# A mixture of eight experts computed for the chosen tokens only, in tiles of 128, between the half steps of an attention loop

## The chip, the cores and the metric

The kernel runs on one NeuronCore of one Trainium2 chip, in float32 throughout. The metric is the device time of one execution in microseconds (us), lower being better. Engines are named as the profile names them: PE multiplies matrices (PEld is its loading of weights), DVE and POOL work element by element, ACT evaluates functions and copies, and SP only issues transfers. POOL also issues the transfers that gather or scatter rows by a list of row numbers. Each engine works through its own instructions in order.

## The reference

There are eight sequences (batches) of 512 tokens with 256 channels. Cut to its parts, the reference is

```python
x = x + over_heads(masked_attention(x))         # stage A: 16 heads; then attention among the heads of one token
y = mixture(x)                                  # stage B, first mixture
x = x + second_mixture(layernorm(y + mha(y)))   # stage B: 16 heads of 16; stage C: one of 8 experts per token

def mixture(x):                                 # T = 4096 tokens, E = 8, two experts per token
    scores = softmax((x @ wt.T + repeat(g @ wg.T, 512)) / 2)
    w, idx = top_k(scores, 2);  w = w / (w.sum(-1) + 1e-20)
    up = leaky(x @ w_gate[e]) * (x @ w_up[e])    # for each e: 256 -> 128, leaky slope 0.01
    y_all[e] = up @ w_down[e]                    # 128 -> 256
    y = sum of w[t, c] * y_all[idx[t, c], t] over c = 0, 1
    return y + (leaky(x @ sw_gate) * (x @ sw_up)) @ sw_down   # a shared expert, width 256
```

The second mixture has its own router, experts of width 512 with a ReLU, and a layernorm after the sum.

## The kernel before

The kernel has three stages, each with its own pools of tiles, one after another.

**Stage A** is the masked attention and the attention among a token's heads ("over-heads"). A flag read at run time picks one of two programs. The mask keeps keys only in the last quarter of a sequence here, so `late_keys` (from line 733) runs: 16 units, each one sequence and half the heads, whose steps are written out by hand. Into their gaps `aside` pulls steps of an iterator `side` (line 981), which is `over_heads_here` (801): one over-heads piece for a row common to most tokens, then `rest` (793), which stores x for the first three quarters of every sequence, then `over_heads()`, which takes pieces from the list `oh_todo` until it is empty. A piece (`one_over_heads`, 187) is 128 tokens in 29 steps: a few matmuls, and 16 large products on POOL (line 244), each followed by a reduction on DVE (247). `hand_over` (332) puts the last 128 tokens of a sequence on the list after stage A has computed them, for the first `BESIDE` = 3 sequences; the other five are worked off in stage B. x after stage A lies in device memory as columns 0 to 255 of `rows_d`.

**Stage B** is the first mixture and 16-head self-attention. `begin(b)` (1300) prepares a batch. `experts` (1246) transposes its tokens, `route` (1173) computes scores and a weight for every token and expert, zero except for two, and then the shared expert and all eight experts are applied to all 512 tokens (`gated`, 1207; products at 1211, 1218 and 1272), each result multiplied by its weight and added into y by DVE (1275). The weights of all experts are loaded once, at the start of the stage. `begin` goes on with the transposed y, the values and the first group's queries and keys. The attention is the loop over 256 half steps, 32 for a batch: a head group `n` of four heads takes eight. In each half step `both` (1365) issues four score matmuls side by side in the array, two for a row maximum (`nmz`, DVE, 1338) of a later group and two whose exponential (`pT_s`, ACT, 1363) is taken; `gather` (1377) multiplies exponentials and values; `divide` (1400) sends sums of the softmax through device memory and back, four small transfers on SP, and multiplies; `end` (1422) is the output projection, layernorm and the second router, whose choice `hand_on_to` scatters into a list of tokens by expert.

The order is by hand. After each half step's attention work, the loop pulls as many steps of `side`, the chained `begin(b)` of all later batches at 38 steps each, as a table `room` gives for that place in the batch; `late`, the left over-heads pieces, gets three or four steps. `begin(0)` and two projections run before the loop. All PSUM tiles of the side work share three banks (`ps_m`).

**Stage C** is the second mixture in the sparse form: tokens sorted by expert in tiles of 256; each tile's tokens gathered from `rows_d` by POOL with a list that SP has loaded (1594, 1597), its expert's weights loaded by SP (1606 to 1610) at an address read from a table in a register, the results scattered to the output. The table is computed by 22 small DVE instructions from the number of tokens for each expert.

Of the kernel before, what the change touches and what calls it, by code (L numbers as in the profile page):

```python
# [24 lines left out]
E = 8  # L25
# [6 lines left out]
ROW = 2 * D + 16  # L32
LAST = NT - 1
BESIDE = 3
# [3 lines left out]
def tile_adaln_attn_ffn(ctx: ExitStack, tc: tile.TileContext, a: dict, out: bass.AP):  # L38
# [67 lines left out]
    rows_d = dram.tile([B * S, ROW], F32, name="rows", tag="rows")  # L106
    w_chosen = mid.tile([P, KD, 12], F32, name="wr", tag="wr")
# [18 lines left out]
    )  # L126
    sofar = mid.tile([P, NT + 1, E], F32, name="sofar", tag="sofar")
    nc.gpsimd.memset(sofar, 0.0)

# [57 lines left out]
    def one_over_heads(i, b, row=None):  # L187
# [4 lines left out]
        if row is None:  # L192
            rows = slice(b * S + i * P, b * S + (i + 1) * P)
            cn = ohp.tile([P, D], F32, name="cn", tag="cn", bufs=3)
            nc.sync.dma_start(cn, cn_d[rows, :])
            xi = ohp.tile([P, D], F32, name="xi", tag="xi", bufs=2)
            nc.sync.dma_start(xi, a["x"][b, i * P : (i + 1) * P, :])
        else:
            cn = row
# [78 lines left out]
        nc.sync.dma_start(rows_d[rows, 0:D], xo)  # L278
        oh_done[b] += 1
# [52 lines left out]
    def hand_over(i, b, pc, mv, rs):  # L332

        cn = ohp.tile([P, D], F32, name="cn_out", tag="cn", bufs=3)
# [398 lines left out]
    def late_keys():  # L733


        with ExitStack() as ph:
# [56 lines left out]
            def rest(b):  # L793
# [4 lines left out]
                nc.sync.dma_start(rows_d[b * S : b * S + LAST * P, 0:D].rearrange("(t p) c -> p t c", p=P), xi)  # L798
                oh_done[b] += LAST

            def over_heads_here():
# [5 lines left out]
                yield from over_heads()  # L807
# [196 lines left out]
            for _ in chain(prep, side, over_heads()):  # L1004
# [25 lines left out]
    def first_max(pool, src, rank, tag):  # L1030
# [4 lines left out]
        oh = pool.tile([p, n, w], F32, name="fm_o" + tag, tag="fm_o" + tag)  # L1035
# [5 lines left out]
        return oh, m  # L1041

    def choose(wk, ps, tag, xT):
# [14 lines left out]
        def best(l, rank, tag):  # L1058
# [9 lines left out]
            return first_max(wk, l, rank, tag)  # L1068
# [51 lines left out]
    with ExitStack() as ph:  # L1120
# [24 lines left out]
        wge, wue, wde = [], [], []  # L1145
        for e in range(E):
            wge.append(wload(f"wge{e}", a["w_gate"][e], P))
            wue.append(wload(f"wue{e}", a["w_up"][e], P))
            wde.append(load(f"wde{e}", [P, D], a["w_down"][e]))
# [16 lines left out]
        v_sets = [wp.tile([P, NT, H * VW + 32 - VW], F32, name=f"v{u}", tag=f"v{u}") for u in range(2)]  # L1166
# [6 lines left out]
        def route(b, xT):  # L1173

            gb = wk.tile([64, P], F32, name="gb", tag="gb")
# [16 lines left out]
            o1, m1 = first_max(wk, sc, rank8, "1")  # L1192
            s2 = wk.tile([P, NT, E], F32, name="r_s2", tag="r_s2")
            nc.vector.scalar_tensor_tensor(s2, o1, -2.0, sc, ALU.mult, ALU.add)
            o2, m2 = first_max(wk, s2, rank8, "2")
# [4 lines left out]
            nc.vector.tensor_tensor(m1, m1, den, ALU.mult)  # L1200
            nc.vector.tensor_tensor(m2, m2, den, ALU.mult)
            nc.vector.tensor_tensor(o1, o1, bc(m1, 2, E), ALU.mult)
            nc.vector.tensor_tensor(o2, o2, bc(m2, 2, E), ALU.mult)
            nc.vector.tensor_tensor(o1, o1, o2, ALU.add)
            return o1

        def gated(xT, wg_, wu_):
# [4 lines left out]
            hh = wk.tile([P, S], F32, name="hh", tag="hh", bufs=3)  # L1212
# [25 lines left out]
        x1 = {}  # L1238

        def load_x1(b):  # L1240
            x1[b] = wk.tile([P, NT, D], F32, name="x1", tag="x1")
            r = b * S
            assert oh_done[b] == NT
            nc.sync.dma_start(x1[b], rows_d[r : r + S, 0:D].rearrange("(t p) c -> p t c", p=P))

        def experts(b, y):

            xT = transposed(wk, ps_m, x1.pop(b), "x1T", ps_tag="m")
            yield
            cw = route(b, xT)  # L1250
            yield
            hs = []
            for c in range(2):
                h = yield from gated(xT, swg[:, :, c * P : (c + 1) * P], swu[:, :, c * P : (c + 1) * P])
                hs.append(h)
# [10 lines left out]
            for e in range(E):  # L1266
                h = yield from gated(xT, wge[e], wue[e])
                for u in range(2):
# [533 lines left out]
```

## Time and profile before

| | us |
|---|---|
| median of three runs (2145.59 to 2154.9) | 2146.6 |
| the profiled execution | 2142.55 |
| its span, first to last instruction | 2140.8 |
| PE busy | 1746.2 (82%) |
| DVE busy | 1104.6 (52%) |
| POOL busy | 536.5 (25%) |
| ACT busy | 502.0 (23%) |

The core's mean granted PE clock is 0.887 of full speed. In a row of the profile, "out<-in" names the tiles written and read, "x" the count, then come busy time in us, the mean of one in ns, and after the bar the idle time of the engine just before these instructions with what ended it. A float32 matrix product appears as two MATMUL records. Busy PE time counts overlapped records once.

### The profile page before, as it was taken

The numbers are of one execution on the slowest core, as the hardware profiler recorded it, in microseconds if no ns is written. First come the engines' busy times: TensorE is split into PE (matmuls) and PEld (weight loads), VectorE is DVE, ScalarE is ACT, GpSimd is POOL, SyncE is SP. The second block draws the span as 40 slices with busy tenths as digits, with TensorE's granted clock in tenths as the row PEclk, the third lists the DMA queues.
The fourth block names the chain that finished last, engine by engine and source line by source line (L and its number), as shares of the span: only waits on it lengthen the run. The fifth ranks groups of instructions, "written<-read, shape, count | busy, mean of one in ns | idle before, by whom it ended". The sixth has DMA issues, their size and how long they took to land.

```text
span 2140.8 us, 21024 instructions
## 1 busy us (share of the span) xinstructions
PE 1746.2 (82%) x7552; PEld 903.4 (42%) x7552; DVE 1104.6 (52%) x2563; ACT 502.0 (23%) x887; POOL 536.5 (25%) x539
## 2 busy tenths in 40 slices
PE   4898224899899988998999999999998885476775
PEld 3665113443343433443444344444443322465664
DVE  4865441456666554564555565564555441343433
ACT  1444000012222122322222323322323322010000
POOL 2510560013233320020010010010010022277677
PEclk9999556969999989999999999998998978688887
DMA  4210005000000000000000000000000000444441
GB/s 133 62 53 13 10 19 146 0 3 18 6 13 4 3 14 11 2 12 11 2 1 22 2 1 12 2 2 12 2 1 12 2 12 4 141 145 145 150 134 49
DMA packets 92145, 74.22 MB, mean 35 GB/s; under 512 B 36285, under 2 KB 81853, under 8 KB 92032
## 3 DMA queue, kind: packets, MB, share of 16 engines
q1 hardware_dynamic: 75200, 58.49, 9.1%
q0 software_dynamic: 6912, 12.88, 2.0%
q10 hardware_dynamic: 9920, 1.42, 0.4%
q8 instruction: 61, 1.00, 0.2%
q14 instruction: 52, 0.43, 0.1%
HBM read 61.95 MB, written 16.42 MB: 37 GB/s over the span
## 4 chain that ended last, share of the span: by engine, by line
PE 61%; DVE 13%; POOL 11%; DMA 6%; issue 4%; ACT 1%; SPq 1%; POOLq 0%; DVEq 0%; ACTq 0%
PE pss L1335 12%; PE pg L1211 6%; PE po_s L1384 6%; PE pu L1218 5%; PE pd L1272 5%; POOL pr L244 4%; DVE nmz L1338 3%; PE pq_s L1289 3%; PE px_s L1428 2%; PE pk_s L1295 2%; PE pst L1359 2%; PE py L1654 2%; DMA sums<-oT_s 2%; DMA xg<-rows,ids_j 2%; PE prs L1418 2%
## 5 line engine op out<-in xcount | busy, mean ns | idle before, releaser
L1338 DVE TENSOR_REDUCE nmz<-pss 128x2 f32<-128x1024 f32 x256 | 311.9, 1220 | 228.9 <-PE pst L1359 192.7
L1363 ACT ACTIVATE pT_s<-pst 128x1024 f32<-128x1024 f32 x256 | 261.8, 1024 | 593.4 <-PE pst L1359 593.4
L1335 PE MATMUL pss<-k_s,q_s 32*128 32x512 f32 x1024 | 327.5, 685 | 69.1 <-DVE nmz L1338 68.6
L1359 PE MATMUL pst<-q_s,k_s 32*128 32x512 f32 x1024 | 310.1, 676 | 1.9 <-DVE nmz L1338 1.6
L1433 POOL TENSOR_TENSOR y<-y,bo_bc 128x256 f32<-128x256 f32 x32 | 23.2, 725 | 838.1 <-DVE y L1432 838.1
L1335 PEld LDWEIGHTS pss<-k_s,q_s 32*128 32x128 f32 x1024 | 86.2, 193 | 260.3 <-DVE nmz L1338 119.8
L1384 PE MATMUL po_s<-pT_s,v 128*32 128x512 f32 x1024 | 157.4, 626 | 4.5 <-ACT pT_s L1363 4.5
L244 POOL TENSOR_TENSOR pr<-qk 128x512 f32<-128x512 f32 x72 | 88.5, 1263 | 211.4 <-DVE fm_r L1039 117.7
L1272 PE MATMUL pd<-wde,hh 128*128 128x256 f32 x512 | 127.4, 392 | 15.5 <-DVE hh L1219 14.6
L1211 PE MATMUL pg<-x1T,wge 128*128 128x512 f32 x256 | 126.0, 616 | 5.2 <-DVE q_s L1351 2.7
L1275 DVE SCALAR_TENSOR_TENSOR y<-pd,fm_o,y 128x256 f32<-128x256 f32 x256 | 109.6, 478 | 37.6 <-PE pd L1272 36.7
L1218 PE MATMUL pu<-x1T,wue 128*128 128x512 f32 x256 | 122.4, 600 | 0.0
L1272 PEld LDWEIGHTS pd<-wde,hh 128*128 128x128 f32 x512 | 94.1, 192 | 63.7 <-DVE hh L1219 32.5
L244 POOL TENSOR_TENSOR pr<-at,v_h 128x512 f32<-128x512 f32 x72 | 89.2, 1275 | 97.7 <-DVE at L259 74.1
L1654 PE MATMUL py<-w,h_e 128*128 128x256 f32 x368 | 108.2, 460 | 0.0
L1214 DVE TENSOR_TENSOR hh<-hh,pg 128x512 f32<-128x512 f32 x80 | 54.6, 683 | 95.5 <-ACT hh L1213 95.4
L1654 PEld LDWEIGHTS py<-w,h_e 128*128 128x128 f32 x368 | 86.8, 242 | 15.7
L1213 ACT ACTIVATE hh<-pg 128x512 f32<-128x512 f32 x80 | 47.7, 597 | 194.4 <-PE pg L1211 185.0
L1628 PE MATMUL pt_j<-ident,xg 128*128 128x128 f32 x92 | 21.9, 347 | 87.0 <-DMA xg<-rows,ids_j 86.9
L1359 PEld LDWEIGHTS pst<-q_s,k_s 32*128 32x128 f32 x1024 | 80.9, 191 | 22.3 <-issue 13.1
L1639 PE MATMUL ph<-xTj,w 128*128 128x256 f32 x368 | 85.1, 385 | 0.8 <-DVE xTj L55 0.8
L1639 PEld LDWEIGHTS ph<-xTj,w 128*128 128x128 f32 x368 | 71.0, 193 | 11.3 <-DVE xTj L55 1.2
(266 smaller groups left out, 2564.5 us busy)
## 6 DMA issues: line engine op xcount, KB each, us to landing
w<-in_w_dram SPq DMA_DIRECT2D x46, 512.0 KB
rows<-xr SPq DMA_DIRECT2D x8, 544.0 KB
x<-rows SPq DMA_DIRECT2D x8, 512.0 KB
x_rest<-in_x_dram SPq DMA_DIRECT2D x8, 384.0 KB
rows<-x_rest SPq DMA_DIRECT2D x8, 384.0 KB
b<-in_b_dram SPq DMA_DIRECT2D x23, 128.0 KB
wq<-in_Wq_dram SPq DMA_DIRECT2D x1, 1024.0 KB
wo<-in_Wo_dram SPq DMA_DIRECT2D x1, 1024.0 KB
```

Of the source, the lines that this page charges most:

```text
L244: nc.gpsimd.tensor_tensor(pr, x, y, ALU.mult)
L1211: nc.tensor.matmul(pg, wg_[:, k, :], xT[:, k, :], start=(k == 0), stop=(k == KD - 1))
L1218: nc.tensor.matmul(pu, wu_[:, k, :], xT[:, k, :], start=(k == 0), stop=(k == KD - 1))
L1272: nc.tensor.matmul(pd[:, t, :], h[:, q : q + P], wde[e], start=True, stop=True)
L1275: nc.vector.scalar_tensor_tensor(yt, pd[:, t, :], cw[:, 2 * u + t, e : e + 1], yt, ALU.mult, ALU.add)
L1335: nc.tensor.matmul(pss[:, u, :], qs[n][r, t * P : (t + 1) * P], ks[n][r, :], start=True, stop=True)
L1338: return lambda: nc.vector.tensor_reduce(nmz[n % 2].rearrange("p t (h r) -> p t h r", h=4)[:, t, 2 * pr : 2 * pr + 2, HD], pss, AX.X, ALU.max,
L1359: nc.tensor.matmul(pst[:, u, :], ks[n][r, c * P : (c + 1) * P], qs[n][r, :], start=True, stop=True)
L1363: return lambda: nc.scalar.activation(pT, pst, AF.Exp)
L1384: nc.tensor.matmul(pos[n][hd * 32 : hd * 32 + 32, :], v_sets[b % 2][:, c, (4 * g + hd) * VW : (4 * g + hd) * VW + 32], ws[hd // 2][:, hd % ...
L1639: nc.tensor.matmul(ph_, w1[:, k, c * P : (c + 1) * P], xT[:, k, :], start=(k == 0), stop=(k == KD - 1))
L1654: nc.tensor.matmul(py[:, u, :], h[:, c, u * P : (u + 1) * P], w2[:, c, :], start=(c == 0), stop=(c == 3))
```

## The change

The first mixture takes the form that stage C has. Work is done for groups of two batches (1024 tokens, `GB` = 2).

- `route(b)` loads x of its batch, transposes it and computes scores as before, then each token's two experts and weights, the places of these choices in lists by expert, and scatters the token numbers into the group's list `ids1_d`, eight scatters of 128 numbers on POOL.
- `TILE1` is 128, `WAIT` 4 and `PAIRS` 12. `mixture(q)` computes a table (`table`, now shared with stage C) and goes through 24 tiles of 128 places, two at a time, 12 pairs. For each pair, `fetch` loads two lists and the weights of two experts (768 KB, eight transfers on SP, no longer resident) and gathers 2 x 128 token rows (POOL), two pairs ahead; `turn` transposes, `widen` multiplies by gate and up weights, `narrow` by the down weights and stores the result to `y1_d`. The number of tiles is fixed; tiles beyond the filled ones are computed too.
- `experts(b)` keeps the shared expert and then gathers each token's two results by eight gathers on POOL, adding them with their weights on DVE.
- x after stage A goes to a second place, `x1_d`, one tensor for each group.
- Before the loop: `route(0)`, `route(1)`, `mixture(0)`, `begin(0)` and two projections, one after another. In the loop, `side` is a plan: `begin(1)`, `route(2)`, `route(3)`, `mixture(1)`, `begin(2)`, `begin(3)` and so on, spread evenly toward a half step by which each `begin` must be done. A `begin` is 14 steps, a `route` 5, a `mixture` 31. All head groups' projections are at the same place in the loop now.
- `BESIDE` becomes 4, and stage A's `side` no longer ends when its list is empty, but goes on looking.
- Some rings of buffers become shorter (cn, hh, pT_s, oT_s), the values' ring longer.

The diff, cut to its core:

```diff
-BESIDE = 3
+GB = 2
+TILE1 = 1 << TILE1_BITS
+TILES1 = ((2 * GB * S - E) // TILE1 + E + 1) // 2 * 2
+BESIDE = 4
...
@@ one_over_heads, rest
         nc.sync.dma_start(rows_d[rows, 0:D], xo)
+        r = b % GB * S + i * P
+        nc.sync.dma_start(x1_d[b // GB][r : r + P, :], xo)
...
@@ over_heads_here
-                yield from over_heads()
+                while True:
+                    yield from over_heads()
+                    yield
...
@@ weights of stage B
-        for e in range(E):
-            wge.append(wload(f"wge{e}", a["w_gate"][e], P))
-            wue.append(wload(f"wue{e}", a["w_up"][e], P))
-            wde.append(load(f"wde{e}", [P, D], a["w_down"][e]))
...
@@ route
+            load_x1(b)
+            yield
+            xT = x1Ts[b] = transposed(wk, ps_m, x1.pop(b), "x1T", bufs=2, ps_tag="m")
+            yield
...
+            nc.tensor.matmul(pr, before, both_e, start=True, stop=False)
+            nc.tensor.matmul(pr, every, sf[:, 0:NT, :], start=False, stop=True)
...
+            for c in range(2):
+                for t in range(NT):
+                    sc_ = nc.gpsimd.indirect_dma_start(
+                        out=ids1_d[q],
+                        out_offset=bass.IndirectOffsetOnAxis(ap=pi[:, c, t : t + 1], axis=0),
+                        in_=token_id[:, bl, t : t + 1],
...
+        def mixture(q):
+            steer, _, first = table(wp, bank, sofar1[:, q, 0, :], e_base1, TILES1, TILE1_BITS, "m_")
...
+            def fetch(j):
+                xg = xg1[j % len(xg1)]
+                w = wk.tile([P, 2, 2, KD, P], F32, name="w_gu", tag="w_gu")
+                wd = wk.tile([P, 2, D], F32, name="w_dn", tag="w_dn", bufs=3)
+                for u in range(2):
+                    i = 2 * j + u
+                    e = nc.sync.value_load(steer[0:1, 0, i : i + 1], min_val=0, max_val=E - 1)
+                    r0 = nc.sync.value_load(steer[0:1, 1, i : i + 1], min_val=0, max_val=places1 - TILE1)
...
+                        nc.sync.dma_start(ids, ids1_d[q][bass.ds(r0, TILE1), :])
+                    nc.gpsimd.indirect_dma_start(
+                        out=xg[:, u, :],
...
+                    for c, src in enumerate(("w_gate", "w_up")):
+                        nc.sync.dma_start(
+                            w[:, u, c], a[src][bass.ds(e, 1)].rearrange("e (k p) m -> p (e k) m", p=P)
+                        )
+                    nc.sync.dma_start(wd[:, u], a["w_down"][bass.ds(e, 1)].rearrange("e m d -> (e m) d"))
...
+            for j in range(2):
+                fetch(j)
+            for _ in range(WAIT):
+                yield
+            turn(0)
+            yield
+            for j in range(PAIRS):
+                widen(j)
+                yield
+                if j + 2 < PAIRS:
+                    fetch(j + 2)
+                if j:
+                    narrow(j - 1)
+                if j + 1 < PAIRS:
+                    turn(j + 1)
+                yield
+            narrow(PAIRS - 1)
+            yield
...
@@ experts
-            for e in range(E):
-                h = yield from gated(xT, wge[e], wue[e])
...
+            for t in range(NT + 1):
+                if t < NT:
+                    yg[t] = wk.tile([P, 2, D], F32, name="yg", tag="yg")
+                    for c in range(2):
+                        nc.gpsimd.indirect_dma_start(
+                            out=yg[t][:, c, :],
...
@@ the loop
-        for _ in chain(begin(0), project(1)):
+        for _ in chain(route(0), route(1), mixture(0), begin(0), project(0), project(1)):
             pass
...
+        for q in range(B // GB):
+            plan.append((64 * q + 16, begin(2 * q + 1), BEGIN))
+            if q + 1 < B // GB:
+                plan += [(None, route(GB * q + GB + u), ROUTE) for u in range(GB)]
+                plan.append((None, mixture(q + 1), MIX))
+                plan.append((64 * q + 48, begin(2 * q + 2), BEGIN))
...
-            due += room[j % 32] * (sum(room) / sum(room[:22]) if j < 22 else 1)
-            while done < due * per_batch / sum(room) and done < per_batch * (B - 1):
-                next(side, None)
+            due += max([(c - due) / (by - j) for by, c in goals if by > j and c > due], default=0.0)
+            while done < due - 1e-6:
+                assert next(side, "end") != "end"
                 done += 1
```

## The prediction, made before the change was run

> **What bounds the kernel now.** I read the busy time of each engine by stage first, cut where the trace shows a border (columns: stretch, length, busy time and count on PE, PEld, DVE, ACT and POOL, granted clock, DMA share, GB/s):
>
> ```profile
> 217.00:316.00 99.00, 22.68 (x52) 11.25 (x50) 45.41 (x81) 3.62 (x10) 63.14 (x56) 0.52 0.03 7
> 316.00:347.00 31.00, 0.00 (x0) 0.00 (x0) 0.16 (x1) 0.00 (x0) 0.00 (x0) 0.50 0.85 231
> 347.00:449.00 102.00, 92.77 (x286) 48.32 (x286) 49.06 (x97) 10.28 (x18) 1.45 (x2) 0.88 0.05 15
> 449.00:1786.00 1337.00, 1235.00 (x5464) 539.89 (x5462) 741.53 (x1455) 371.95 (x463) 197.64 (x209) 0.94 0.03 7
> ```
>
> Stage A's units end at 217; until 316 three leftover over-heads pieces run alone, 33 us each. Then 31 us of weight loading in which no engine works, 102 us for batch 0's mixture and first projections, 1337 us of loop, and stage C, which the change does not touch. In the loop PE is busy 1235 of 1337. The same view by batch (borders at every 32nd exponential of the loop):
>
> ```profile
> 448.00:690.00 242.00, 223.50 (x831) 99.18 (x832) 149.21 (x275) 55.81 (x79) 81.15 (x67) 0.92 0.04 10
> 1220.00:1378.00 158.00, 153.84 (x720) 69.89 (x720) 91.50 (x185) 47.94 (x59) 13.93 (x18) 0.98 0.02 5
> 1683.00:1786.00 103.00, 86.36 (x422) 30.19 (x420) 43.67 (x88) 35.65 (x40) 13.79 (x18) 0.87 0.03 7
> ```
>
> A middle batch leaves PE 4 us idle: PE sets the pace, with DVE at 58%. The last batch, whose side work is done, takes 103 us. The first takes 242, because over-heads pieces run in it. Next, the groups of the dense experts, and one of their weight loads:
>
> ```profile
> L1272 PE MATMUL pd<-wde,hh 128*128 128x256 f32 x512 | 127.4, 392 | 15.5 <-DVE hh L1219 14.6
> L1211 PE MATMUL pg<-x1T,wge 128*128 128x512 f32 x256 | 126.0, 616 | 5.2 <-DVE q_s L1351 2.7
> L1218 PE MATMUL pu<-x1T,wue 128*128 128x512 f32 x256 | 122.4, 600 | 0.0
> L1272 PEld LDWEIGHTS pd<-wde,hh 128*128 128x128 f32 x512 | 94.1, 192 | 63.7 <-DVE hh L1219 32.5
> ```
>
> Matmuls overlap, so I price them by back-to-back runs in the timeline and the chain of waits. A product appears as two records.
>
> ```profile
> 1244.04 1.98 PE L1211 MATMUL pg<-x1T,wge 128*128 128x512 f32 x4
> 96.69 1.06 PE L900 MATMUL pss<-kT,qT 65*128 65x128 f32 x8
> 96.25 0.60 PE L946 MATMUL pst<-ident,s 128*128 128x128 f32 x4
> ```
> ```profile
> 388.92 1.99 PE pd L1272 x8
> 221.30 9.76 POOL pr L244 x8
> 1832.12 8.68 DMA ids<-token_id,pi
> ```
>
> Four records of 512 columns take about 1.92 us (1.98 with their lead-in), eight of 256 the same (0.24 each), one of 128 columns 0.133, a transpose 0.15.
>
> **Part 1, the loop's PE work.** An expert over a batch is 3 x 1.92 = 5.76 us, eight are 46 us; in the loop seven batches lose 322 us of PE. Added: three mixtures of 12 pairs, each pair with 4 transposes (0.6), 16 widening records of 128 columns (2.13) and 4 narrowing records of 256 (0.96): 3.7 us, so 44 per mixture, 133 in all. Six routings add about 1 us each of placing matmuls; one over-heads piece fewer takes off about as much. PE: 1235 - 322 + 133 = 1046.
>
> [...] The records of the experts load 128 columns in 192 ns, longer than 0.133 us. At 0.192 a pair is 4.6 us and the loop 34 us longer. But the eight records above had their own weight loads and took 1.06 us; I take the row, and keep 34 for the range.
>
> **Part 2, idle PE in the loop.** It is 102 us now. DVE loses 8 x 3.3 = 26 us a batch (products and accumulations of 0.69, 0.69 and 4 x 0.48 us) and gains some 12, so it does not become the bound. SP, POOL and the transfers get new work. SP waits a great deal today:
>
> ```profile
> SPq L1409 <- ACT oT_s L1403: 859.6, 31, 66.1
> ```
>
> so issue time is to be had, but the queue is in order. The nearest case is stage C's first tile:
>
> ```profile
> 1840.81 0.41 SPq L1594 DMA_DIRECT2D ids_j<-ids  x1
> 1843.82 1.05 POOL L1597 DMA_INDIRECT xg<-rows,ids_j  x1 [10.73 <-DMA ids_j<-ids]
> 1850.45 0.45 PE L1628 MATMUL pt_j<-ident,xg 128*128 128x128 f32 x1 [23.16 <-DMA xg<-rows,ids_j]
> ```
>
> List to gather 3.0 us, gather to transpose 6.6. A pair's fetch is eight SP issues at about 0.55 us plus four register loads (some 0.8 us per two): 6 us. The second tile's list sits behind the first tile's weights, which wait for the widening two pairs back: 2.3 + 3 + 6.6 = 12 us until its transposes, against three side steps at 1.08 a half step, 2.8 half steps of about 4.7 us (the 1215 below over 256): 13 us. So it is hidden, barely; I charge nothing, and if the cover goes each microsecond late costs 36.
>
> The start of a mixture is not covered. Eight scatters take POOL 10 us (1.28 each); the last lands 8.7 us after issue in the chain above (up to 17 with other traffic). The list load waits for all, with SP's queue behind it: the loads of the softmax sums (which PE waits for), weights and x1. The program gives it two steps, 8 us. SP falls some 15 us behind, and I charge 15 for each of three mixtures, 45. [...]
>
> At POOL, `end`'s additions queue behind gathers and scatters, and DVE's statistics behind those: 10 us. The load of x1 moves to one step, some 4 us, ahead of its transposes; alone it took 5 us and the issue before that 1, so I charge 2 for each of six routings, 12. The gathers of results (2.6 us of POOL per 128 tokens, 2.1 to land, a step of 4.4 ahead) are about hidden. Idle is then 102 + 45 + 10 + 12 = 169, and the loop 1046 + 169 = 1215: 122 less. Bounds: idle unchanged, 189 less; 3 us late per pair more, 14 less. I take the reckoned one, 122, since the latencies in it are rows.
>
> The first group's projection, moved out of `begin` to where the others stand, is the same eight records and costs nothing. Neither do the smaller rings (cn, hh, pT_s, oT_s): the gather that frees a pT_s stands ahead in PE's own order. If that cover failed it would be ACT's 1.0 us per half step.
>
> **Part 3, stage A's tail.** The endless side iterator picks the pieces up as soon as they are handed over, ten steps per unit; four pieces of 29 steps fit between units 4 and 16. The 99 us tail goes. But a piece brings DVE about 15 us (16 reductions of 0.68 and some ten small ones). The units with a piece beside them, 48 to 87, took 13 us each, the later ones (130 us for some 15) 8.7. Twelve units at 4.3 more are 51. Stage A ends at about 265 instead of 316: 51 less; bounds 25 and 75. The fourth piece's loads and stores and the second store of x (some 0.5 us of SP each) lie under the same units; bare they would be 20 us.
>
> **Part 4, the prologue.** It is serial, with no attention over it. Weights: 3 MB and 24 issues less bring x1 17 us after stage A instead of 31. First routing: transposes 3, logits 4, vector chain 5, placing 3; the second adds about 14; its scatters 10, landing 9: 48 us (66 if sixteen scatters queue at 3 us each); I take 57. List, gather, transposes, copy 12. The mixture runs at SP's and the buffers' pace: 12 us of part 2's latency plus 2.4 of widening for two pairs, 7 a pair; PE's own 3.7 and SP's 6 are lower bounds. 12 x 7 = 84, less overlap at its ends: 80. Then the shared expert 14, gathers left over 7, and 33 from the transposes to the first exponential as now. 17 + 57 + 12 + 80 + 21 + 33 = 220 against 449 - 316 = 133: 87 more. Bounds 60 and 110.
>
> **Sum.** New list initialisations at the start +2; tail -51, prologue +87, loop -122: -84. The profiled execution took 2142.55 us (span 2140.8, 1.75 around it), so 2058; the median of the runs shown is 2146.6, 4 above the profiled one, within their scatter. I predict 2058.
>
> **Rivals.**
> - Queues hide everything: idle stays near 102, prologue +65: 2142.5 - 189 + 65 - 60 = 1958. For it: SP's 860 us of waiting. Against it: the list load's wait for scatters.
> - Late pairs eat most of it: 1.5 us per pair, 54: 2112. For it: barely covered gathers.
> - Slower: every gather comes late, because SP stands in the waits of the softmax sums or of a store when its turn comes and PE's in-order queue stops at the transposes. From (2142.5 - 2058) / 36 = 2.3 us per pair it decides; at 4 us, 144, the time is 2202. For it: stage C's gathers, which end up on the chain at 2 to 7 us.
> - The change does not do what it says: PE pays the weight load and PE's work is not halved: 34 more, 2092; still faster.
>
> **How the numbers follow.** Forecast, with 2092 in its neighbourhood, 0.46, all hidden 0.18, mostly eaten 0.16, slower 0.20. What a measurement of this kernel tells from no change is about 0.5%, 11 us. The slower rival and the edge of the eaten one put 0.19 above 2157 and 0.07 within 11 us of 2146.6; faster 0.74. The range leaves out about a tenth at each end: 1955 to 2165; the forecast's own is 2015 to 2105.
>
> **What would show it.** The stretch of POOL products with PE idle after stage A gone; some 220 us from there to the first pT_s; 256 exponentials within 1215 us; PE idle waits on xg1 transposes small and on the softmax sums grouped at mixture starts. Wrong if pt_1's idle time passes 100 us in the loop, a pair in the prologue is far from 7 us, or stage A's units stretch beyond 13 us.

## The result and the profile after

The changed kernel takes 2176.04 us (median of four runs, 2168.25 to 2177.98) against 2147.51 for the kernel before on the same chip: a ratio of 1.012, with a 95% interval of 1.008 to 1.016. It is slower by 1.2%. I had forecast 2058. The profiled execution took 2168.25 us, its span is 2166.5.

Cut at the same borders as before (end of stage A's units in the kernel before, first weight load of stage B, the wait for the first gathered rows, first exponential, last exponential), the stages of the changed kernel are (stretch, length, busy time and count on PE, PEld, DVE, ACT and POOL, granted clock, DMA share, GB/s):

```profile
217.00:300.00 83.00, 58.86 (x222) 37.16 (x222) 57.48 (x184) 25.22 (x103) 38.41 (x32) 0.71 0.04 12
300.00:344.00 44.00, 16.82 (x68) 15.44 (x68) 15.55 (x59) 1.63 (x4) 14.98 (x21) 0.50 0.53 129
344.00:375.00 31.00, 2.15 (x7) 1.69 (x7) 5.14 (x33) 0.00 (x0) 9.87 (x11) 0.50 0.36 61
375.00:518.70 143.70, 103.64 (x412) 70.21 (x413) 34.14 (x55) 22.91 (x43) 34.24 (x34) 0.76 0.37 106
518.70:1819.50 1300.80, 1084.48 (x5412) 505.74 (x5412) 634.18 (x1310) 388.89 (x508) 352.23 (x364) 0.87 0.20 49
```

Stage A's lone pieces are gone (PE is busy 59 of the 83 us that were its tail), but the units themselves now last until 299. The loop does 151 us less PE work and is only 36 us shorter: PE's idle time in it is 216 us instead of 101. Set against the forecast, with differences of the two profiled executions:

| us | forecast | measured |
|---|---|---|
| stage A, to the first weight load of stage B | -51 | -16 (316.0 to 300.2) |
| prologue, from there to the first exponential | +87 | +86 (132.6 to 218.5) |
| loop, first to last exponential | -122 | -36 (1336.8 to 1300.8) |
| stage C and the rest | 0, start +2 | -8 (355.4 to 347.0; 344 to 356 in the runs here) |
| sum | -84 | +26 |

By batch (borders at every 32nd exponential; batches 2, 3, 4, 5 and the last):

```profile
926.50:1110.90 184.40, 142.66 (x807) 76.62 (x808) 75.82 (x186) 55.44 (x79) 54.09 (x58) 0.85 0.41 90
1110.90:1257.90 147.00, 134.43 (x669) 61.63 (x668) 82.07 (x167) 46.94 (x58) 30.61 (x34) 0.93 0.09 27
1257.90:1446.50 188.60, 145.38 (x807) 77.86 (x808) 75.85 (x185) 55.60 (x79) 53.81 (x58) 0.84 0.39 83
1446.50:1595.70 149.20, 128.04 (x614) 54.94 (x616) 73.06 (x128) 45.68 (x55) 26.50 (x30) 0.90 0.07 19
1716.00:1819.50 103.50, 86.78 (x424) 30.15 (x420) 43.29 (x88) 35.45 (x39) 13.82 (x18) 0.87 0.03 7
```

The even batches, beside which a group is routed and its mixture runs, leave PE idle for some 42 us each; the middle batches of the kernel before left 4 to 9. The odd ones, with little side work, leave 13 to 21. The last batch, without any, is as before.

The groups of new work in the changed kernel, with what ended the idle time before them:

```profile
L1382 PE MATMUL pg<-xT,w_gu 128*128 128x128 f32 x768 | 117.1, 315 | 10.7 <-ACT xT L1373 10.2 <-issue 0.4
L1351 POOL DMA_INDIRECT xg<-x,ids_j x96 | 97.3, 1014 | 309.6 <-DMA ids_j<-ids 204.9 <-PE pt L1372 29.4 <-PE py L1395 19.1
L1311 POOL DMA_INDIRECT ids<-token_id,pi x64 | 63.0, 984 | 154.1 <-DVE pi L1307 119.3 <-issue 15.8 <-DVE m_n_i L173 10.1
```

The chain behind the idle time can be read in the timeline of one mixture start (start, duration, engine, line; in brackets the idle time ahead and what ended it):

```profile
1288.46 0.98 POOL L1311 DMA_INDIRECT ids<-token_id,pi  x1 [18.34 <-DVE pi L1307]
...
1297.45 0.98 POOL L1311 DMA_INDIRECT ids<-token_id,pi  x1 [0.31 <-issue]
1298.44 0.74 POOL L1665 TENSOR_TENSOR y<-y,bo_bc 128x256 f32<-128x256 f32 x1
...
1299.21 0.43 DVE L85 BATCH_NORM_STATS2 ln_st<-y 128x6 f32<-128x256 f32 x1 [7.21 <-issue]
...
1302.91 1.22 PE L1567 MATMUL pss<-k_s,q_s 32*128 32x512 f32 x2 [6.93 <-DVE nmz L1570]
...
1308.02 0.34 SPq L1350 DMA_DIRECT2D ids_j<-ids  x1
...
1312.58 1.06 POOL L1351 DMA_INDIRECT xg<-x,ids_j  x1 [7.43 <-DMA ids_j<-ids]
```

Eight scatters hold POOL for 10 us. `end`'s bias addition stands behind them, DVE's statistics behind that (DVE stood 7.2 us), the row maxima `nmz` behind those in DVE's queue, and PE's scores behind `nmz` (PE stood 6.9 us). SP issues the first list only 10.6 us after the last scatter; the last 3.4 us of that it stands for the scatters' landing. Some 60 us later a list comes late: PE stands 11 us at the transposes of gathered rows, and the softmax sums, which share SP's queue with lists and weights, hold DVE 11 us at the same time:

```profile
1357.49 0.00 SPq L1350 DMA_DIRECT2D ids_j<-ids  x1
...
1371.45 1.05 POOL L1351 DMA_INDIRECT xg<-x,ids_j  x1 [9.70 <-DMA ids_j<-ids]
...
1375.03 0.90 PE L1372 MATMUL pt<-ident,xg 128*128 128x128 f32 x3 [11.05 <-DMA xg<-x,ids_j]
1375.26 0.25 DVE L1644 RECIPROCAL sums<-sums 128x16 f32<-128x16 f32 x1 [11.18 <-DMA sums<-sums]
```

This list was issued 14.0 us ahead of its gather. Of the 72 lists in the loop three took 11 to 14 us from issue to gather, the others at most 6; the median is 3.0. The late ones come at two places, each within 3 us after four scatters of the second router (L1187) on POOL, and lists are as late at the same two places in `lists_first` and `no_scatter` below. What delays them there no run shows.

Where PE's idle time in the loop ends, in the changed kernel (two rows) and in the kernel before:

```profile
L1567 PE MATMUL pss<-k_s,q_s 32*128 32x512 f32 x980 | 322.5, 709 | 104.7 <-DVE nmz L1570 96.0 <-issue 8.7
L1372 PE MATMUL pt<-ident,xg 128*128 128x128 f32 x144 | 26.4, 298 | 47.9 <-DMA xg<-x,ids_j 40.4 <-DVE q_s L1583 7.4
L1335 PE MATMUL pss<-k_s,q_s 32*128 32x512 f32 x980 | 312.5, 673 | 67.3 <-DVE nmz L1338 66.8 <-ACT k_s L1297 0.4
```

Of PE's idle in the loop, 96 us end with `nmz` (67 in the kernel before), 40 with gathered rows (none before) and 23 with `xr` of `end` (13 before); these are gaps between PE's records, by what released the next one. The first is a symptom: whatever stops DVE ends as a wait for `nmz`. Of the 40, 21 are the two places of the late lists, and 9 the first mixture in the loop, whose lists stood behind the scatters' landing.

### The profile page after: what moved, and what is told of

Same layout as the page of the kernel before. It is cut to its first block, busy times and chain, and to the rows that moved or that the text cites. A ratio compares the mean times of both kernels' runs of the same rounds, so it can differ in the third digit from the quotient of the medians.

```text
span 2166.5 us, 24074 instructions
## 1 busy us (share of the span) xinstructions
PE 1638.3 (76%) x7720; PEld 918.4 (42%) x7720; DVE 1026.4 (47%) x2491; ACT 535.4 (25%) x967; POOL 770.4 (36%) x769
## 4 chain that ended last, share of the span: by engine, by line
PE 36%; issue 12%; DMA 10%; POOL 9%; DVE 8%; SPq 3%; ACT 1%; POOLq 0%; DVEq 0%; ACTq 0%
PE pss L1567 9%; PE po_s L1616 4%; DVE nmz L1570 3%; PE pg L1382 2%; DMA xg<-rows,ids_j 2%; PE py L1847 2%; DMA ids_j<-ids 2%; PE pq_s L1522 2%; PE pst L1591 2%; PE pk_s L1528 2%; DMA ids<-token_id,pi 2%; PE px_s L1660 2%; PE prs L1650 1%; PE pv_s L1546 1%; DMA xg<-x,ids_j 1%
## 5 line engine op out<-in xcount | busy, mean ns | idle before, releaser
L1567 PE MATMUL pss<-k_s,q_s 32*128 32x512 f32 x1024 | 337.7, 718 | 106.3 <-DVE nmz L1570 97.5
L1595 ACT ACTIVATE pT_s<-pst 128x1024 f32<-128x1024 f32 x256 | 261.8, 1024 | 507.2 <-PE pst L1591 502.0
L1591 PE MATMUL pst<-q_s,k_s 32*128 32x512 f32 x1024 | 324.4, 717 | 3.2 <-ACT pT_s L1595 1.6
L1351 POOL DMA_INDIRECT xg<-x,ids_j x96 | 97.3, 1014 | 309.6 <-DMA ids_j<-ids 204.9
L1495 POOL DMA_INDIRECT yg<-y,yi x64 | 65.3, 1021 | 259.1 <-DVE y L1507 156.1
L1382 PE MATMUL pg<-xT,w_gu 128*128 128x128 f32 x768 | 117.1, 315 | 10.7 <-ACT xT L1373 10.2
L1382 PEld LDWEIGHTS pg<-xT,w_gu 128*128 128x128 f32 x768 | 109.6, 226 | 36.4 <-ACT xT L1373 18.2
L1311 POOL DMA_INDIRECT ids<-token_id,pi x64 | 63.0, 984 | 154.1 <-DVE pi L1307 119.3
L1372 PE MATMUL pt<-ident,xg 128*128 128x128 f32 x192 | 37.7, 307 | 98.2 <-DMA xg<-x,ids_j 87.9
L1847 PE MATMUL py<-w,h_e 128*128 128x256 f32 x368 | 100.6, 435 | 0.0
L1387 DVE TENSOR_TENSOR hh<-hh,pg 128x256 f32<-128x256 f32 x48 | 20.1, 418 | 165.4 <-ACT hh L1386 147.8
```

The costliest lines, as they stand in the source:

```text
L1311: sc_ = nc.gpsimd.indirect_dma_start(out=ids1_d[q], out_offset=bass.IndirectOffsetOnAxis(ap=pi[:, c, t : t + 1], axis=0), in_=token_id[:, ...
L1351: nc.gpsimd.indirect_dma_start(out=xg[:, u, :], out_offset=None, in_=x1_d[q], in_offset=bass.IndirectOffsetOnAxis(ap=ids, axis=0), bounds_ ...
L1382: nc.tensor.matmul(pg[:, c, u, :], w[:, u, c, k, :], xT[:, k, u, :], start=(k == 0), stop=(k == KD - 1))
L1495: nc.gpsimd.indirect_dma_start(out=yg[t][:, c, :], out_offset=None, in_=y1_d[grp], in_offset=bass.IndirectOffsetOnAxis(ap=yi[:, c, t : t + ...
L1567: nc.tensor.matmul(pss[:, u, :], qs[n][r, t * P : (t + 1) * P], ks[n][r, :], start=True, stop=True)
L1591: nc.tensor.matmul(pst[:, u, :], ks[n][r, c * P : (c + 1) * P], qs[n][r, :], start=True, stop=True)
```

## The experiments

Times are medians; the ratio, with its 95% interval, is to the kernel before measured beside it, which took 2143 to 2150 us. The changed kernel's own ratio is 1.012 (1.008 to 1.016). Loop times, PE busy and idle are read between the first and the last of the 256 exponentials of one profiled execution, which can lie 10 us from the median (`bo_dve`: 2153 and 2163).

### The stage A part alone

The kernel before, with only the part that touches stage A:

```diff
-BESIDE = 3
+BESIDE = 4
...
-                yield from over_heads()
+                while True:
+                    yield from over_heads()
+                    yield
...
-            for _ in chain(prep, side, over_heads()):
+            side.close()
+            for _ in over_heads():
```

> The kernel before with the part of the change in stage A alone: BESIDE is 4 and stage A's side iterator goes on looking for pieces; the dense first mixture stays. If stage A gains what the changed kernel's trace shows (its weights start at 300 us instead of 316) and the loop loses one over-heads piece of some 17 us, the time is about 2143 - 33 = 2110 us, and the mixture costs the changed kernel some 60 us. If stage A gains the 51 us of the prediction, it is about 2075. If the four pieces beside the units bring nothing, it is 2125 or more.

Measured 2104.0, ratio 0.983 (0.979 to 0.987). Stretches: stage A's old tail, prologue, loop:

```profile
217.00:300.00 83.00, 57.38 (x217) 35.65 (x215) 56.88 (x181) 25.21 (x103) 38.40 (x34) 0.71 0.05 11
300.00:434.30 134.30, 95.99 (x285) 50.60 (x286) 49.28 (x97) 9.93 (x18) 2.28 (x5) 0.78 0.23 63
434.30:1753.90 1319.60, 1227.33 (x5446) 537.05 (x5446) 728.54 (x1429) 370.52 (x458) 177.16 (x192) 0.94 0.03 7
```

The first exponential comes 14 us earlier, not 51, but the loop is 17 us shorter as well: one piece fewer runs beside batch 1 (PE 8 us less, idle 9 us less). Another 11 us lie in stage C and after it, which this edit does not touch. This part gains some 40 us, and the sparse mixture therefore costs about 70 (72 by the medians, 69 by the profiled executions): its prologue takes 84 us more than this kernel's, and its loop takes off only 19, because 143 us less of PE busy time come with 124 us more of idle.

### Single stalls

`bo_dve`, the bias of `end` off POOL:

```diff
-                nc.gpsimd.tensor_tensor(yt, yt, bo_bc, ALU.add)
+                nc.vector.tensor_tensor(yt, yt, bo_bc, ALU.add)
```

> The changed kernel with one edit: the addition of bo_bc in end moves from POOL to DVE (32 instructions, 0.42 us each on DVE instead of 0.74 on POOL). Theory of POOL's queue (this addition stands behind eight scatters or behind gathers that wait for their lists, DVE's statistics stand behind it, the row maxima behind those, and PE waits): DVE's waits for POOL at the statistics, 50 us in the loop, go, PE's idle time before pss falls from 96 to 60 or less, and the time falls by 35 to 60 us, to about 2125. Theory of SP and the transfers (lists, weights and sums late): within 10 us of 2172.

2163.2, ratio 1.010 (1.006 to 1.013). The profiled loop is 15 us shorter (idle for `nmz` 79 instead of 96), and DVE's waits for the softmax sums are longer (112 us instead of 95). By the ratios the gain is 5 us, which is not clear of noise; the theory's 35 to 60 did not come.

`lists_first`: in `fetch`, both tiles' lists and gathers are issued ahead of the four gate and up loads and the two down loads, instead of tile by tile.

> The changed kernel with one edit: a fetch issues the list loads and gathers of both tiles first and then the weights of both, so that the second list no longer stands behind the first tile's weights. Theory of SP and the transfers: PE's waits for gathered rows fall from 40 us in the loop to 15 or less and a pair before the loop from 7.2 us to about 6, together 35 to 50 us less, 2130. Theory of POOL's queue: POOL waits less for the lists in the loop (164 us now) and some of the pss idle goes too, but most of the 35 us per group that stand behind scatters stay: 15 to 25 us less, 2150.

2150.0, ratio 1.002 (1.000 to 1.004), the largest gain of a single edit. Idle for gathered rows fell from 40 to 5 us, `nmz` rose to 106: at the place of the late list shown above, PE now waits 6 us for `nmz`. The prologue did not change, so this part of the expectation failed:

```profile
519.00:1803.00 1284.00, 1092.91 (x5412) 506.79 (x5412) 634.17 (x1310) 388.07 (x508) 352.36 (x364) 0.87 0.20 50
```

`spread`, scatters two to a step (`ROUTE` 8 instead of 5):

```diff
                     alone_id(sc_, q)
-            yield
+                    if t % 2:
+                        yield
```

> The changed kernel with one edit: the eight scatters of a routing come two to a step over four steps instead of all in one (a routing is 8 steps then). Theory of POOL's queue: end's addition gets between them, so its longest wait of 7 to 12 us at the start of a mixture goes and PE's idle before pss falls by 20 us or more in the loop: 2150. Theory of SP: the list loads wait for the last scatter a little longer, so 2172 or up to 15 us more.

2192.3, ratio 1.022 (1.019 to 1.025): slower. PE's idle in the loop falls (216 to 208), but its busy time grows from 1084 to 1112. That the three more steps press the others together is a guess.

`lists_late`, three empty steps between the table and the first `fetch`:

```diff
+            for _ in range(3):
+                yield
             for j in range(2):
                 fetch(j)
```

> The changed kernel, with three empty side steps put between a mixture's table of tiles and its first list loads. Theory (SP and POOL stand behind the landing of the last scatters: in the changed kernel POOL waited 9.7 us for a list at 1361 us and SP's first list load came 10.6 us after the last scatter): two such stands per mixture, three mixtures in the loop, each worth some 5 to 10 us of TensorE's idle, so the loop loses 15 to 40 us and the run takes 2130 to 2155. Rival (the stand is short beside the whole idle time, and three more steps press the other side steps closer): 2165 to 2180.

2178.5, ratio 1.014 (1.012 to 1.017): the rival's time. PE's idle in the loop did fall by 20 us (216 to 197), as the theory has it, but PE's busy time of the same 5412 records rose by 26 (1084 to 1111), so nothing was won.

`weights_by_act`: `lists_first`, and the mixture's weights through ACT's queue (the register load too):

```diff
-                        nc.sync.dma_start(
+                        nc.scalar.dma_start(
                             w[:, u, c], a[src][bass.ds(e, 1)]...
```

> The changed kernel, with both tiles' lists and gathers issued ahead of the pair's weights, and the weights loaded through ScalarE's queue in place of SP's. Theory (the divisors `sums` stand in SP's queue behind the weights, VectorE behind `sums`, TensorE behind VectorE): against lists first alone (2150 us, TensorE idle 106 us for `nmz` in the loop) VectorE's waits for `sums` fall from 95 us towards the 51 us of the kernel before, TensorE's idle for `nmz` falls below 70 us, and the run takes 2105 to 2130. Rival (six issues and two register loads a pair stand before the exponentials on ScalarE, and its queue waits for the weights' buffers): TensorE's idle moves from `nmz` to the exponentials and the run takes 2150 or more.

2182.1, ratio 1.015 (1.012 to 1.018): the rival's time. The theory's first step came true, idle for `nmz` fell to 63 us, and so did the rival's: idle for exponentials is 57 us instead of 5.

`no_dead_loads`: the changed `begin` still loads the next batch's x1, which no one reads any more; without it:

```diff
-            if b + 1 < B:
-                load_x1(b + 1)
```

> The changed kernel without the load of the next batch's x1 that `begin` still issues and nobody reads (seven loads of 512 KB). Theory (with one buffer for x1, SP stands in front of these loads until the routing's transposes are done, and they stand before later lists, weights and `sums`): 5 to 15 us off, 2153 to 2163. Rival (nothing that TensorE waits for is behind them): 2165 to 2172.

2163.9, ratio 1.008 (1.005 to 1.010): 12 us by the medians and 10 by the ratios, as the theory had it. My prediction has no term for these loads.

`three_edits`, `bo_dve`, `lists_first` and this one together:

> The changed kernel with the three edits together: both lists and gathers of a pair ahead of its weights (alone 2150), the bias of `end` added on VectorE (alone 2163), no dead loads of x1 (alone 2164). Theory (separate stalls, gains add): 2176 - 26 - 13 - 12 = 2125, between 2115 and 2135, TensorE's idle in the loop 216 - 45 or less. Rival (one stall uncovers the next): 2143 to 2155, idle 190 or more.

2143.1, ratio 0.998 (0.995 to 1.001), idle 196: the rival's range. By the medians 33 us came of 51; by the ratios 29 of 36, and that shortfall is within the noise. In the profiled loops idle fell by 20 us, where the three alone took 25, 13 and 14, so there the gains overlap, with one profile each. `end_off_pool` takes the layer norm's two steps (`xr`) off POOL too, beside the bias:

> The changed kernel with all of the end of a batch's additions and multiplications by the layer norm's vectors on VectorE (the bias of `y`, and the two steps of `xr`), so that no work of `end` stands behind scatters or gathers on POOL. Theory (the scatters' 45 us in the loop are this stand): idle in the loop falls from 216 to some 170, `pt_x2T` from 23 to below 10, the run takes 2120 to 2145. Rival (the bias alone gave 13 us, and VectorE's own 14 us more a batch take back the rest): 2155 to 2170.

2169.4, ratio 1.010 (1.003 to 1.017): the rival. Nothing of `end` stands behind scatters any more, and PE's idle in the loop is still 206 us, 53 of it for gathered rows, 12 more than in the changed kernel.

### What the scatters and the gathers cost

`no_scatter` leaves out the scatters, `no_scatter_gather` the lists' loads and the gathers of rows too (in both the routed experts' part of the output is left out, and the multiplications run on old or zero rows).

> The changed kernel without the 64 scatters of token numbers (so the lists of places stay empty, and the gathers fetch no rows: the mixture's result is left out, all its other instructions run). My prediction put 45 us on the scatters in the loop, three groups at 15. Theory (scatters are the stall: POOL is held for 10 us twice per mixture, and lists wait for their landing): TensorE's idle in the loop falls from 216 to some 160, before the loop some 20 us go, and the run takes 2090 to 2120. Rival (routing, tables, pairs and gathers are late by themselves): idle in the loop 190 or more, the run 2135 to 2160.

> The changed kernel without the scatters, the lists' loads and the gathers of rows (the mixture multiplies zeros; its result is left out). Theory (in `no_scatter` the gathers of rows still held TensorE for 32 us in the loop and some 25 us before it): idle in the loop 163 - 35 = 130, first exponential at 475 to 485 us, the run 2040 to 2065. Rival (POOL and the gathers are not what the pairs wait for; the weights, 1.25 MB a pair through SP, are): 2090 or more.

2106.5 (0.979; 0.975 to 0.982) and 2062.9 (0.960; 0.954 to 0.966). Their loops:

```profile
503.00:1759.30 1256.30, 1092.79 (x5412) 506.17 (x5412) 634.74 (x1310) 388.35 (x508) 304.44 (x316) 0.87 0.18 46
```
```profile
484.90:1707.50 1222.60, 1078.31 (x5412) 501.63 (x5412) 633.93 (x1310) 387.70 (x509) 231.91 (x244) 0.88 0.17 47
```

In these profiles the scatters cost 44.5 us of loop and 16 ahead of it; lists and gathers 34 and 18. By the medians it is 70 and 44, so how the sum divides is known to some 10 us. In `no_scatter` the loop moves 46 GB/s over 1256 us, some 6 MB less than the changed kernel's 49 over 1301, and the rows of the chosen tokens are 6.3 MB: gathers from empty lists fetched about no rows, so some of the scatters' share is shorter gathers. PE's idle in the loop falls from 216 to 164 and then 144, its busy time goes from 1084 to 1093 and then 1078. Together it is 112 us, more than the whole loss: with token lists and gathered rows left out, the changed kernel is 4% faster than the one before. (The weights of a pair are 768 KB, not the 1.25 MB expected above.)

### Pauses and the granted clock

`before_stalls` is the kernel before with ten additions of a scratch tile on DVE (0.69 us each) in each of the 32 units, 7 us each time:

```diff
             assert pm == pr
+            if j % 8 == 4:
+                for _ in range(10):
+                    pin(nc.vector.tensor_tensor(scr, scr, scr, ALU.add))
             both(m, t, n, i, pr)
```

> The kernel before with a pause of 7 us put on VectorE once a unit (ten additions of a scratch tile, 0.68 us each, ahead of the maxima of half step 4 of each of the 32 units), and nothing else changed: TensorE runs the same instructions. Theory (the granted clock falls after pauses): TensorE's idle in the loop rises by 80 to 200 us, the granted clock there falls from 0.94 to 0.90 or less, and TensorE's busy time of the same instructions rises from 1235 by 25 to 60 us. Rival (the change's own transfers and instructions set the clock): busy time within 10 us of 1235, clock 0.93 or more.

2263.0, ratio 1.052 (1.046 to 1.059). The loop of the kernel before, and this one:

```profile
448.60:1785.40 1336.80, 1235.40 (x5464) 540.11 (x5464) 741.53 (x1455) 371.75 (x462) 197.64 (x209) 0.94 0.03 7
```
```profile
457.70:1915.40 1457.70, 1296.70 (x5464) 563.02 (x5464) 932.90 (x1775) 371.08 (x463) 198.44 (x209) 0.90 0.03 7
```

The same 5464 PE records take 61 us more, and the clock fell from 0.94 to 0.90; idle rose by 60, less than I had expected. The pauses cost twice here: 60 us as idle and 61 as longer busy time. The work that DVE has in them is not the cause as such: the changed kernel has less DVE work than the kernel before (634 us in the loop, 742) and the lower clock.

The clock recorded with the profiles has two levels in the loop, 1.0 and 0.5, and the half-speed stretches that begin in the loops of the kernel before and the changed one last 3.41 us or a multiple of it, up to 23.9. In the changed kernel 16 widening records (L1382) took 3.78 us at clock 0.50 (at 437 us, ahead of the loop) and 2.05 at 1.00 (at 1446). As an estimate, half of PE's busy time inside the stretches is what the clock takes:

| loop of | half-speed stretches | taken from PE's busy time | busy time without that |
|---|---|---|---|
| the kernel before | 23, 165 us | 77 us | 1158 us |
| `before_stalls` | 35, 285 us | 129 us | 1168 us |
| the changed kernel | 36, 340 us | 129 us | 956 us |

So by this estimate 52 of the 61 us are the clock. PE pauses of over 1 us (gaps in the union of PE's records) are 48 in the kernel before and 44 in `a_only` (clock 0.94), 67 here (0.90), 68 in `no_scatter` and 74 in the changed kernel (both 0.87): of these five loops the ones with more pauses have the lower clock, but 67 and 68 pauses go with 0.90 and 0.87, so their number alone does not tell it.

### The first group dense

`dense_first` computes the experts of batches 0 and 1 as the kernel before does, from resident weights, and the mixture of the other three groups loads its weights over them (a ring shorter here and there to make room):

```diff
+            yield from (experts_dense if b < GB else experts)(b, y)
...
-        for _ in chain(route(0), route(1), mixture(0), begin(0), project(0), project(1)):
+        for _ in chain(begin(0), project(0), project(1)):
```

> The changed kernel with the experts of batches 0 and 1 computed densely as in the kernel before, from resident weights, and the sparse mixture only for the groups of batches 2 and 3, 4 and 5, 6 and 7, its weight tiles loaded over the resident ones. Theory (the prologue's 84 us come from the first mixture running alone, and only from that): the time to the first exponential falls from 218 us after stage A to some 140, the loop grows by the 46 us of dense experts of batch 1 (322 us over seven batches), and the run takes 2168 - 80 + 46 = 2134, between 2120 and 2150. Rival (dense steps and the first mixture are squeezed into the same half steps, so the loop's idle grows by another 30 us or more): 2160 and above.

2201.1, ratio 1.027 (1.023 to 1.030). The first exponential comes at 432.5 us, 86 us earlier, so the prologue's loss is the first mixture's, as the theory says. But the loop grew by 114 us, and PE's busy time by 112, where the theory had 46. PE's idle stays at 219 us, but 72 of it are now waits for down weights, which are loaded too early over those still to be used. With a place for each of four pairs:

```diff
-                s0, d0 = 2 * (j % 2), 2 * (j % 3)
+                s0 = d0 = 2 * (j % 4)
```

> As `dense_first`, but each pair of the sparse mixture takes its own two of the eight resident weight tiles, pair j the places 2(j mod 4): in `dense_first` the down weights of pair j + 2 were loaded over those of pair j - 1 ahead of its multiplication, which therefore waited for that load (TensorE idle 72 us in the loop for it, and multiplied by the wrong pair's weights). Theory: that idle goes, the time to the first exponential stays near 132 us after stage A, and the run takes 2201 - 60 = 2125 to 2145. Rival (the idle only moves to the gathered rows or to `nmz`, as it did in the other runs): 2165 or more.

2125.8, ratio 0.989 (0.984 to 0.994), at the low end of the theory's range. Two more versions on top:

> As `dense_first4`, with three edits more that helped or were neutral alone: both lists and gathers of a pair ahead of its weights, the bias of `end` added on VectorE, no dead loads of x1. Theory (the idle times are apart from one another, so the gains add: 18 + 13 + 4 us): 2095 to 2115, as good as the beside-part alone (2104). Rival (the late thing after each edit is another one, so the three together give no more than the best alone, 18 us): 2115 to 2130, or more if `dense_first4` itself stays above 2145.

> `dense_first4` with lists and gathers ahead of the weights and nothing of `end` on POOL. Theory (POOL's queue holds both the end and the gathers): 2126 - 25 = 2085 to 2110, as good as or better than the beside-part alone (2104). Rival (as with the three edits together: the next late thing takes over): 2115 to 2130.

2129.2 (0.991; 0.987 to 0.995) and 2117.7 (0.985; 0.979 to 0.991): the rival both times. They beat the kernel before, as `a_only` does, and none of them beats `a_only` at 2104; the last cannot be told from it by the ratios (0.985 and 0.983).

## Why the prediction was wrong

The forecast gain of 84 us became a loss of 26. Of these 110 us, 38 are PE's busy time in the loop, 47 its idle time there and 35 stage A; 1 in the prologue and 10 in stage C and the start go the other way.

**Part 1, PE's work in the loop, was 38 us short as time, though not as work.** The step that failed is carrying the 1235 over as measured, with the clock that it had, and adding 133 at full speed; the sum was 1046, and it took 1084. By the estimate from the clock record, PE's busy time at full speed fell by 203 us (1158 to 956), where 322 - 133 = 189 were forecast. But half-speed stretches took 129 us of it instead of 77. So the 38 are 52 for the clock less 14 for the work. In `before_stalls`, where pauses are the only edit, the same 5464 records took 61 us more, 52 of them by the same estimate.

The price of 0.192 us a record, by the time of a weight load, which I had set aside and kept for the range, did not hold: 16 widening records, each with its own weight load, took 2.05 us, 0.128 each, as in the row that I took.

```profile
1446.32 2.05 PE L1382 MATMUL pg<-xT,w_gu 128*128 128x128 f32 x16
```

Long pauses alone do not account for the half-speed stretches. Pauses over 3 us are 4 in the loop of the kernel before, 11 in `before_stalls` and 15 in the changed kernel, and in both of the latter the half-speed stretches took, by the estimate, 52 us more of PE's busy time than in the first. Of the 34 stretches that begin in the loop of `before_stalls`, 23 have no pause over 3 us in the 6.8 us (two of the record's 3.41) ahead of them; the 34 last 7.7 us on average.

**Part 2, idle PE, was 169 and is 216.** The step that failed is "so it is hidden, barely; I charge nothing", on the pairs' lists and gathers. PE's waits that end with gathered rows are 40 us in the loop, and without lists and gathers the loop is 34 us shorter, 19 in idle and 15 in busy time. Spread over 36 pairs that is 0.9 us each, but it is not spread: a list is usually gathered by 3.0 us after its issue, as I had it, and 21 of the 40 us come from two places where this took 13 and 14. The 13 us of cover held for most pairs and not for these.

The term that I feared most came out near its number: three groups of scatters at 15 us, 45; without them the loop is 44.5 us shorter and PE's idle 53 less. That is in part luck. I had put it on SP, 15 us behind at each start, but in the whole loop SP stood 15 us for the scatters' landing and 46 for the table of tiles, which I had not counted; and some of the 44.5 is shorter gathers.

```profile
SPq L1346 <- DVE m_of_t L193: 46.1, 3, 31.3
SPq L1350 <- DMA ids<-token_id,pi: 15.3, 4, 8.3
```

By which path the scatters cost what they do stays open, since taking `end` off POOL (`end_off_pool`) and fetching later (`lists_late`) brought little or nothing. `end` behind POOL, priced at 10, gave 5 to 15 in `bo_dve`. The rest of the idle, 43 us above the kernel before's, stands against 22 that I had for `end` and the loads of x1. Last, the batch that I read as leaving PE 4 us idle was the best of the middle ones; the others left 7 to 9.

**Part 3, stage A, was mis-sized.** The pieces cost the units 83 us (217 to 300), some 21 a piece, where I had 51 from the difference of two unit lengths; so 16 of the 51 us came. `a_only`, which is 39 us faster, has 14 of them there and 17 in the loop, where I had counted some 6 us of PE work for the missing piece.

**Part 4, the prologue, was right in sum:** 218.5 against 220. Its parts were off and cancel, so the closeness is in part luck: the first loads 18 us against 17, the routings to the first list load 49 against 57, list to widening 10 against 12, the pairs 87 against 80 (7.3 us a pair against 7), shared expert and gathers 11 against 21, and from there to the first exponential 42 against 33.

**The rivals.** The "late pairs" rival had the mechanism that my forecast lacked, at 1.5 us a pair (0.9 measured, and 18 us more in the prologue). The slower one has the sign, but it needed 2.3 us a pair from that mechanism alone, and that did not happen: PE's busy time (38), its idle (47) and stage A (35) used the gain up together, and none of them alone turns the sign.

Open: which part of the 43 us of idle that remain above the kernel before's with neither scatters nor gathers belongs to the weights, the result gathers and the routing; what delays a list to 14 us; and what the first scatter of a group would cost with an idle POOL.

## What to carry to other kernels

Taking work off the bounding engine pays only as far as the work that replaces it arrives on time: here, against `a_only`, 143 us less of PE time brought 124 us more of pauses, and PE's granted clock fell from 0.94 to 0.87. A chain of list, gather and multiply should be priced with its slowest transfers too, not with the usual latency and an average step: here 3.0 us was usual, and 14 set the longest waits. And measure a change's parts alone: the small part was worth 39 us, and the large one lost about 70.

## What the hardware showed that I had not expected

In `before_stalls`, 60 us more idle in the loop came with 61 us more busy time in the same records, 52 of them by the estimate from the clock record: the pauses cost about their own length again, and 23 of the 34 half-speed stretches that begin there have no pause over 3 us in the 6.8 us ahead. A list of 128 numbers can be late: the median from issue to gather was 3.0 us, and at two places of the loop it took 13 and 14. Scattered lists of 4-byte numbers landed slowly here: in the prologue SP stood 12.6 us in front of its first list load for the last of sixteen scatters of 128 numbers. POOL issued that scatter 5.4 us into the wait, so the landing took 7.1 us; in the loop one took 8.0. POOL itself waited between scatters for earlier ones to land, 5.0 us in two waits:

```profile
360.42 0.97 POOL L1311 DMA_INDIRECT ids<-token_id,pi  x1 [0.30 <-issue]
```
```profile
SPq L1350 <- DMA ids<-token_id,pi: 12.6, 1, 12.6
```
```profile
POOL ids L1311 <- DMA ids<-token_id,pi: 5.0, 2, 3.6
```
